# A convolution-attention and Mamba stack on one core: the last depthwise part and the last norms in turn, and the second scan step's input read from SBUF

## The chip, the core and the metric

The kernel runs on one core of a Trainium2 chip: TensorE (PE in the profile, with its weight loads as PEld), VectorE (DVE), ScalarE (ACT), GpSimd (POOL) and SyncE (SP), which share an on-chip memory (SBUF), with PSUM for the results of matmuls and HBM as main memory. Each engine runs its own instructions in order. An instruction that needs another engine's result waits on a semaphore, and everything behind it on its engine waits with it. The metric is the time of one execution in microseconds, taken on the device; less is better.

## The reference

The input is an image of 64 x 64 points with 256 channels. Layer 0 is a convolution-attention block, layer 1 a bidirectional Mamba block with an expert layer behind it:

```python
x = x + conv_attention(group_norm(x))
t = tokens(x)
t = t + mamba_both_ways(layer_norm(t))
t = t + experts(layer_norm(t))
```

For the convolutions and the attention:

```python
qkv = concat(conv1x1(x), conv3x3(x), conv5x5(x))      # q, k, v: 256 channels each
qkv = depthwise3x3(qkv)
q, k = l2norm(q), l2norm(k)                           # over the 32 channels of a head
o = softmax(q @ k.T * temperature) @ v                # 8 heads, 4096 points
```

For the Mamba block, once forward and once over the reversed tokens (u is the normalised input, 512 inner channels, 16 states each):

```python
xc, z = split(u @ in_proj.T)
xc = silu(causal_conv4(xc) + conv_b)
dt, B, C = split(xc @ x_proj.T)
dt = softplus(dt @ dt_proj.T + dt_b)
h = exp(dt * A) * h + dt * B * xc                     # step by step along the tokens
y = (h * C).sum(states) + xc * D
out = (y * silu(z)) @ out_proj.T
```

## The kernel before

All arithmetic is in float32. The kernel works on chunks of 512 points (N), and there are 8 of them (NCH). Channels lie on the 128 partitions, 256 channels as two tiles (CT). Phases follow one another; each has its own pools of SBUF and PSUM, and a pool of the next phase takes over the memory of the last one, so that its first writer waits for that memory's last readers and writers. Inside the phases the order of the instructions is written out by hand (`tc.manual_schedule`).

**The convolutions' end.** `conv_phase` (from about 80 us to 650 us) goes through twelve units (`units`): a kind (k, q or v), a half of the image and a tile of channels. For each one, PE makes the convolution and its result goes to a padded tile (`pad0` and `pad1` in turn). While unit n is convolved, the generator `depthwise` of unit n - 1 is stepped: one step is one multiply-add of DVE (L551), which adds one of nine taps to `acc`; the first tap is made by ACT (L544). The last unit is the v of the lower half, second tile. Of its rows, PE makes 16 (`shared`) by nine diagonal matmuls for each of two pieces (`products`, L520); these stand ahead of the first L551 in the generator. DVE makes the rest in two halves of eight steps. After each half `turn` transposes the result on PE (L618), ACT copies it (L620) and POOL stores it (L621).

The depthwise results of q and k are normalised in groups of up to three chunks, by a chain of callbacks that `later` puts into `events` and `tick` calls, one link a tick:

- `norm_sums`: squares on ACT (L581), sums over the heads on PE (L582)
- `norm_inverse`: maximum on DVE (L589), root on ACT (L590), reciprocal on DVE (L591), and a matmul that brings the result back to all partitions (L596)
- `norm_apply`: a product on DVE (L277) for each chunk, a reordering copy on ACT (L605) and a store by POOL (L609); it then calls `norm_sums` for the next group

When the loop over the units ends, the depthwise part of the last unit (16 steps) is still to be done, and so are two groups of q (three chunks and two), of which the sums of the first stand. The kernel before finishes the first and then the others:

```python
            drain(before)
            while events:
                tick()
```

**Attention.** `attention_phase` begins with loads by SP: the first chunk of q (L901), then k and v in eighths, tile by tile (L892, L893). A first score matmul (L1006) needs the first q and the first eighth of k. The scores and the weighting by them then keep PE busy to about 1930 us. The phase's end makes x1, the residual of layer 0, in chunks.

**The scans.** `mamba_phase` goes through 16 pairs i of a chunk c and a direction d: i = 2c + d. The backward direction (d = 1) takes the chunks from the end, so i = 1 works on chunk 7. Each i has 32 slots, one for each tile of channels, group of states and pair of rows (e, k, j). A slot is one scan on DVE over 1024 elements (L1742) and one product with C (L1747); five slots in 32, the set `POOLED`, have POOL make that product (L1752). Ahead of it, ACT makes exp(dt A) (`decay`, L1719, called da below) and POOL makes dt B xc (`inflow`, L1729, called dbx). ACT also keeps the state (L1773), and PE sums over the states (L1782). After the eight slots of one e, DVE multiplies the sum with z (`close`, L1790).

While the slots of i run, the generator `prepare(i + 1)` makes the inputs of the next one, so many steps in each slot. Its steps, in order: two projections of u into xp (L1303; PE, then copies by ACT, L1331), two more (L1336), four convolutions along the tokens (PE L1349, ACT L1345), Silu (L1353), the projection to dt, B and C (PE L1358, ACT L1361), four projections to dt (PE L1378, ACT L1374 and L1375), an exponential (L1381), a rational step (L1387 to L1394), a logarithm, and pieces of dt that are stored and read again. The projections share two PSUM tiles (`mm`), so the third has to wait for the copy of the first.

How many steps each slot gives is one, except in i = 0, where `LATE` holds them back:

```python
        LATE = {0: 0, 1: 0, 2: 0, 3: 0, 4: 0, 6: 2, 7: 6, 13: 2, 14: 2, 15: 2, 16: 2}
```

For i = 0, u was loaded at the end of attention. The input of i = 1 is the norm of chunk 7, made at the scans' own start by `start()`: the tile `un`, whose last product POOL makes (L138). SP stores it to `ud` (L1634), where i = 14 reads it again, and in the fifth slot `load_u(1)` reads it back from there into the tile `u` (L1312) for `prepare(1)`:

```python
            dt_piece(0, 0, 3, ex)
            load_u(1)
            yield
```

`start()` is itself stepped, once in each of the first slots. In its fifth slot ACT also makes Silu of z (L1642).

**The experts.** `expert_phase` follows from about 3833 us to the end.

Of the kernel before, what the change touches and what calls it, by code (L numbers as in the profile page):

```python
# [61 lines left out]
def step(gen, n=1):  # L62

    for _ in range(n):
        if gen is None or next(gen, StopIteration) is StopIteration:
            return False
    return True


def drain(gen):  # L70
    while step(gen):
        pass
# [28 lines left out]
def layer_norm(cx, pool, new_psum, src, dst, mul=None, rest=0, centred=False):  # L101

    nc = cx.nc
    xc = src
    if not centred:  # L110
        ps = new_psum()
        for t in range(CT):
            nc.tensor.matmul(ps, cx.mean_mat, src[:, t, :], start=t == 0, stop=t == CT - 1)
        yield "DVE"
        xc = pool.tile([P, CT, N], FP, name="ln_xc", tag="ln_xc", bufs=1)
        nc.vector.tensor_tensor(xc, src, ps[:, None, :].to_broadcast([P, CT, N]), ALU.subtract)
    yield "ACT"
    nc.scalar.activation(dst, xc, AF.Square)
    yield "PE"
    ps = new_psum()  # L120
    for t in range(CT):
        nc.tensor.matmul(ps, cx.mean_mat, dst[:, t, :], start=t == 0, stop=t == CT - 1)
    yield "ACT"
    rstd = pool.tile([P, N], FP, name="ln_rstd", tag="ln_rstd", bufs=1)
    nc.scalar.activation(rstd[0:1, :], ps[0:1, :], AF.Identity, bias=cx.eps[0:1, :])
    row = cx.rows.tile([1, N], FP, name="ln_row", tag="ln_row", bufs=2)
    nc.sync.dma_start(out=row, in_=rstd[0:1, :])
    few = pool.tile([P, N // P], FP, name="ln_few", tag="ln_few", bufs=1)
    nc.sync.dma_start(out=few, in_=row.rearrange("o (p j) -> (o p) j", p=P))
    for at in range(1 + rest):  # L130
        yield "POOL" if at == rest else "DMA"
    nc.gpsimd.tensor_tensor(few, few, cx.minus_half, ALU.pow)  # L132
    inv = cx.rows.tile([1, N], FP, name="ln_inv", tag="ln_inv", bufs=2)
    nc.sync.dma_start(out=inv.rearrange("o (p j) -> (o p) j", p=P), in_=few)
    nc.sync.dma_start(out=rstd, in_=inv.to_broadcast([P, N]))
    for at in range(1 + rest):
        yield "POOL" if at == rest else "DMA"
    (mul or nc.vector).tensor_tensor(dst, xc, rstd[:, None, :].to_broadcast([P, CT, N]), ALU.mult)  # L138
    yield "ACT"
# [34 lines left out]
def conv_phase(cx, xT, w1, w3, w5, temp, qd, kd, vd, uk, uv):  # L174
# [17 lines left out]
    with ExitStack() as ctx:  # L192
# [318 lines left out]
        def diagonal(ch):  # L511
            for tap in range(9):
                w_ap = wdw[:, 9 * ch + tap : 9 * ch + tap + 1]
                nc.scalar.activation(diag[:, tap, :], cx.ident, AF.Copy, scale=w_ap)
# [108 lines left out]
        rows_left, busy, events, clock = [], [], [], [0]  # L623
# [4 lines left out]
        def tick():  # L628

            clock[0] += 1  # L630
            due = [f for n, f in events if n <= clock[0]]
            events[:] = [(n, f) for n, f in events if n > clock[0]]
            for f in due:
                f()

        with tc.manual_schedule(engines=ORDERED):
# [95 lines left out]
            before = None  # L732
            for n, (kind, half, t) in enumerate(units):
# [42 lines left out]
                before = depthwise(kind, half, t, pad)  # L776
                if n == len(units) - 2:
                    diagonal(2 * CT + units[-1][2])
            drain(before)
            while events:  # L780
                tick()

# [435 lines left out]
def mamba_phase(cx, early, w_in, w_x, w_out, w1, w2, x1d, ud, bcd, dtd, x2d, u2d, usum):  # L1220
# [12 lines left out]
    with ExitStack() as ctx:  # L1233
# [60 lines left out]
        def mm_psum():  # L1294
            return pmm.tile([P, N], FP, name="mm", tag="mm")
# [13 lines left out]
        def load_u(i):  # L1309
            c, d = divmod(i, 2)  # L1310
            u = early.new_u()
            nc.sync.dma_start(out=u, in_=ud[NCH - 1 - c if d else c])  # L1312
            gots[i] = {"u": u}

        def in_pair(q, e):
            return [in_proj(q % 2, gots[q]["u"], e), in_proj(q % 2, gots[q]["u"], e + 1)]

        def few():
            return sp.tile([P, N], FP, name="few", tag="few", bufs=3)
# [228 lines left out]
        def start():  # L1548


            got, xp = gots[0], early.xp
            x1 = tl.tile([P, CT, N], FP, name="x1", tag="a1b")
            nc.gpsimd.dma_start(out=x1, in_=x1d[NCH - 1])
            un = tl.tile([P, CT, N], FP, name="un", tag="hn")
            norm = layer_norm(cx, tl, tl_psum, x1, un, nc.gpsimd)
            nc.scalar.copy(halo[0], xp[:, :, N : N + 3])
            xc = got["xc"] = pr.tile([P, ET, N], FP, name="xc", tag="xc")
            nc.scalar.activation(xc, xp[:, :, 0:N], AF.Silu)
            for d in range(2):
                nc.scalar.activation(aneg[d], cx.col(f"alog{d}", 0, ET * DS), AF.Exp)  # L1560

                nc.vector.tensor_scalar(aneg[d], aneg[d], -1.0, -1e-30, ALU.mult, ALU.min)
            nx = DR + 2 * DS
            pd = mm_psum()
            for e in range(ET):
                nc.tensor.matmul(pd[0:nx, :], wx[0][:, e, :], xc[:, e, :], start=e == 0, stop=e == ET - 1)
            xd = few()[0:nx, :]
            nc.scalar.copy(xd, pd[0:nx, :])
            nc.sync.dma_start(out=bcd[0], in_=xd[DR:nx, :])
            load_bc(0, 0)  # L1570
            ex = early.wide("ex")[:, :, 0:N]
            dt = got["dt"] = sp.tile([P, ET, N], FP, name="dt", tag="dt")

            def soft(e):
                ps = mm_psum()
                nc.tensor.matmul(ps, wdt[0:DR, P * e : P * e + P], xd[0:DR, :], start=True, stop=True)
                nc.scalar.activation(ex[:, e, :], ps, AF.Abs, bias=cx.col("dtb0", e))
                nc.vector.tensor_scalar(dt[:, e, :], ps, cx.col("dtb0", e), 0.0, ALU.add, ALU.max)
                nc.scalar.activation(ex[:, e, :], ex[:, e, :], AF.Exp, scale=-1.0)

            def rest(e):

                rd = few()
                nc.vector.tensor_scalar(rd, ex[:, e, :], -1.0, -1.0, ALU.mult, ALU.add)
                nc.vector.scalar_tensor_tensor(rd, rd, 1.0, ex[:, e, :], ALU.add, ALU.add)
                nc.vector.tensor_tensor(dt[:, e, :], dt[:, e, :], rd, ALU.add)

            def log(e):
                nc.scalar.activation(ex[:, e, :], ex[:, e, :], AF.Ln, bias=1.0)

            soft(0)
            rest(0)
            log(0)
            for v in range(2):
                dt_piece(0, v, 0, ex, nc.vector)
            load_dt(0, 0, 0)
            load_dt(0, 0, 2)
            load_bc(0, 1)

            step(norm)  # L1600
            step(norm)
            soft(1)
            step(norm)
            soft(2)
            rest(1)
            soft(3)
            step(norm)
            inflow(0)
            decay(0)
            decay(1)  # L1610
            rest(2)
            rest(3)
            step(norm)
            load_bc(0, 2)
            zs = in_pair(0, ET)
            for e in range(1, ET):
                log(e)
            inflow(1)
            step(norm)
            load_bc(0, 3)  # L1620
            yield

            for h in range(2):
                z = sp.tile([P, 2, N], FP, name="z", tag="z", bufs=3)
                got.setdefault("z", []).append(z)
                for f in range(2):
                    nc.scalar.copy(z[:, f, :], zs[f])
                if h == 0:
                    zs = in_pair(0, ET + 2)
                    for v in range(2):  # L1630
                        dt_piece(0, v, 1, ex)
                    yield
            step(norm)
            nc.sync.dma_start(out=ud[NCH - 1], in_=un)  # L1634
            drain(norm)
            yield
            dt_piece(0, 0, 2, ex)
            yield
            dt_piece(0, 1, 2)
            yield  # L1640
            for z in got["z"]:
                nc.scalar.activation(z, z, AF.Silu)  # L1642
            dt_piece(0, 0, 3, ex)
            load_u(1)
            yield
            dt_piece(0, 1, 3)
            yield
# [61 lines left out]
        gots, bcs, dts, m_of, das, us, ys, hs = {}, {}, {}, {}, {}, {}, {}, {}  # L1709
# [87 lines left out]

        AHEAD = 5

        LATE = {0: 0, 1: 0, 2: 0, 3: 0, 4: 0, 6: 2, 7: 6, 13: 2, 14: 2, 15: 2, 16: 2}  # L1800
        LONG = {1, 9, 17, 24}

        FULL = {
# [7 lines left out]
        with tc.manual_schedule(engines=ORDERED):  # L1811
# [5 lines left out]
            for n, (i, e, k, j) in enumerate(slots):  # L1817
# [40 lines left out]
                if i == 0:  # L1858
                    step(begin)
                step(prep, LATE.get(at, 1) if i == 0 else 1)  # L1860
                if at >= SPS - AHEAD and i + 2 < 2 * NCH:
# [347 lines left out]
```

## Time and profile before

| | |
|---|---|
| three runs | 4153.34, 4162.94 and 4164.72 us; median 4162.94 |
| the profiled execution's own time | 4161.68 us |
| its span, first instruction to last | 4159.7 us |
| PE busy | 3626.1 us (87%) |
| DVE busy | 3493.0 us (84%) |
| ACT busy | 2662.3 us (64%) |
| POOL busy | 1748.0 us (42%) |

All times below are microseconds from the start of the span. A line of a timeline gives the start, the time taken, the engine, the line of the kernel, the operation, the result and its inputs with their shapes, and how many instructions are merged in it. In square brackets is the time that the engine was idle before it, and what ended that wait. A float32 matmul of 512 columns stands as two records. A line of SP (SPq) is the issue of a DMA, not the transfer. Where a wait has several causes, the bracket names the one that came last.

### The profile page before, as it was taken

Reading aid. Unit: us, or ns where it says so; the run is one execution under the profiler, and the core shown is the slowest. Engines: PE = TensorE matmul, PEld = TensorE weight load, DVE = VectorE, ACT = ScalarE, POOL = GpSimd, SP = SyncE. Lnnn points to the kernel's source line nnn. Section 1 sums busy time; section 2 is a strip of 40 time slices with the busy share of each in tenths; the row PEclk is TensorE's granted clock in tenths of the full one; section 3 lists DMA queues with packets and bytes.
Section 4 is the critical chain, followed back from the end, with each engine's and each line's share of the span. In section 5 each row is a group of like instructions: output and inputs, shape, how many; then the busy total and the mean of one; then the engine's idle time right before and its main releaser. Section 6 shows DMA issues by size and latency. Waiting matters only on the chain. (4 is left out here: it accounts for less than half of the span.)

```text
span 4159.7 us, 43569 instructions
## 1 busy us (share of the span) xinstructions
PE 3626.1 (87%) x15116; PEld 1187.8 (29%) x15116; DVE 3493.0 (84%) x2898; ACT 2662.3 (64%) x4131; POOL 1748.0 (42%) x1188
## 2 busy tenths in 40 slices
PE   6769997999999999998788888888888888876798
PEld 2223332222222222222222222222222222221343
DVE  8998786889879879778899999999999999998211
ACT  1111226878878878776777778778787877774122
POOL 3020000000000000001888889888888989886000
PEclk9889998999999999999888888998989899987899
DMA  6232214000000000002334344343434334341121
GB/s 207 91 110 94 68 57 136 9 29 19 17 24 19 17 24 19 11 22 86 112 115 127 120 125 130 117 133 112 133 109 123 120 122 142 107 136 65 66 67 39
DMA packets 150533, 351.20 MB, mean 84 GB/s; under 512 B 35493, under 2 KB 44453, under 8 KB 150046
## 3 DMA queue, kind: packets, MB, share of 16 engines
q1 hardware_dynamic: 139214, 313.17, 24.5%
q0 software_dynamic: 11088, 35.14, 2.5%
q8 instruction: 121, 1.98, 0.2%
q14 instruction: 110, 0.90, 0.1%
HBM read 268.69 MB, written 79.56 MB: 84 GB/s over the span
## 5 line engine op out<-in xcount | busy, mean ns | idle before, releaser
L1729 POOL TENSOR_TENSOR dbx<-dtxr,b 128x1024 f32<-128x1024 f32 x512 | 1202.4, 2358 | 197.0 <-DMA dtxr<-dtd 97.0
L1013 ACT ACTIVATE e<-sc 128x1024 f32<-128x1024 f32 x1024 | 992.6, 1023 | 200.6 <-PE sc L1006 161.9
L1742 DVE TENSOR_TENSOR_SCAN da<-da,state,dbx 128x1024 f32<-128x1024 f32 x432 | 1014.3, 2348 | 18.2 <-ACT da L1719 7.2
L932 DVE TENSOR_TENSOR s<-s,e 128x1024 f32<-128x1024 f32 x768 | 880.8, 1221 | 43.3 <-ACT e L1013 42.8
L1719 ACT ACTIVATE da<-dtr,aneg 128x512 f32<-128x512 f32 x1024 | 708.1, 692 | 33.2 <-DMA dtr<-dtd 3.6
L1006 PE MATMUL sc<-q,kS 32*128 32x512 f32 x4096 | 652.8, 643 | 15.3 <-DMA kS<-kd 8.3
L132 POOL TENSOR_TENSOR ln_few<-ln_few,minus_half 128x4 f32<-128x4 f32 x29 | 29.4, 1014 | 1410.0 <-DMA ln_few<-ln_row 1410.0
L1747 DVE TENSOR_TENSOR h<-da,c 128x1024 f32<-128x1024 f32 x432 | 529.2, 1225 | 33.9 <-DVE da L1742 1.4
L939 PE MATMUL av<-e,vT 128*32 128x512 f32 x4096 | 548.4, 606 | 3.7 <-ACT o L945 3.7
L1782 PE MATMUL y<-h,sel 128*32 128x512 f32 x2048 | 377.1, 661 | 95.7 <-DVE h L1747 69.8
L453 PE MATMUL cv<-v,u 128*128 128x512 f32 x928 | 412.9, 605 | 28.4 <-DVE pad L274 14.0
L1303 PE MATMUL mm<-u,win 128*128 128x512 f32 x496 | 272.5, 701 | 85.4 <-ACT state L1773 29.1
L1006 PEld LDWEIGHTS sc<-q,kS 32*128 32x128 f32 x4096 | 211.5, 183 | 460.7 <-issue 235.8
L551 DVE SCALAR_TENSOR_TENSOR acc<-pad,wdw_s,acc 128x768 f32<-128x768 f32 (+1 forms) x192 | 236.2, 1235 | 24.0 <-ACT acc L544 18.3
L453 PEld LDWEIGHTS cv<-v,u 128*128 128x128 f32 x928 | 178.9, 194 | 260.0 <-issue 227.1
L1773 ACT COPY state<-da 128x2 f32<-128x2 f32 x431 | 67.9, 158 | 260.1 <-DVE h L1747 258.9
L1349 PE MATMUL mm<-xp,taps 128*128 128x512 f32 x480 | 213.3, 596 | 0.2 <-DVE m L1498 0.2
L932 DVE TENSOR_TENSOR s<-e 128x1024 f32<-128x1024 f32 x128 | 151.1, 1222 | 66.5 <-ACT e L1013 66.4
L1742 DVE TENSOR_TENSOR_SCAN h<-da,state,dbx 128x1024 f32<-128x1024 f32 x80 | 187.5, 2344 | 9.5 <-ACT state L1773 9.0
L939 PEld LDWEIGHTS av<-e,vT 128*32 128x32 f32 x4096 | 81.2, 108 | 395.5 <-issue 377.1
L1752 POOL TENSOR_TENSOR h<-h,c 128x1024 f32<-128x1024 f32 x80 | 188.3, 2354 | 2.1 <-ACT state L1773 2.1
L1303 PEld LDWEIGHTS mm<-u,win 128*128 128x128 f32 x496 | 106.5, 224 | 252.2 <-issue 109.9
(352 smaller groups left out, 3845.3 us busy)
## 6 DMA issues: line engine op xcount, KB each, us to landing
dtr<-dtd SPq DMA_DIRECT2D x128, 512.0 KB
dtxr<-dtd SPq DMA_DIRECT2D x128, 512.0 KB
b<-bcd SPq DMA_DIRECT2D x64, 256.0 KB
c<-bcd SPq DMA_DIRECT2D x64, 256.0 KB
dtd<-dt SPq DMA_DIRECT2D x64, 256.0 KB
dtd<-few SPq DMA_DIRECT2D x64, 256.0 KB
u<-uv SPq DMA_DIRECT2D x24, 640.0 KB
u<-ud SPq DMA_DIRECT2D x16, 512.0 KB
```

The lines of the kernel that those rows point to most:

```text
L453: nc.tensor.matmul(rows4(ps), u[:, dy, P * ci : P * ci + P], v[:, dy : dy + HR, ci, :], start=dy + ci == 0, stop=dy == k - 1 and ci == CT - 1,
L551: nc.vector.scalar_tensor_tensor(o, src, w_ap, o, ALU.mult, ALU.add)
L932: nc.vector.tensor_tensor(z, x, y, ALU.add)
L939: nc.tensor.matmul(g.av[32 * h : 32 * h + 32, :], vT[:, kb, P * t + 32 * h : P * t + 32 * h + 32], es[h // 2][:, h % 2, :], start=kb == 0, ...
L1006: nc.tensor.matmul(ps[h // 2][:, h % 2, :], kS[r, t, P * kb : P * kb + P], q_t[r, t, :], start=True, stop=True,)
L1013: nc.scalar.activation(e, ps[i], AF.Exp)
L1303: nc.tensor.matmul(ps, win[d][:, t, P * e : P * e + P], u[:, t, ::-1] if d else u[:, t, :], start=t == 0, stop=t == CT - 1,)
L1719: nc.scalar.activation(da[:, v, :], dts[i, e, j][0][:, v, :], AF.Exp, scale=aneg[i % 2][:, a : a + 1])
L1729: nc.gpsimd.tensor_tensor(u, dts[i, e, j][1], bcs[i, k][0][:, None, :].to_broadcast([P, 2, N]), ALU.mult)
L1742: nc.vector.tensor_tensor_scan(das[n].rearrange("p v n -> p (v n)"), da.rearrange("p v n -> p (v n)"), u.rearrange("p v n -> p (v n)"), st ...
L1747: nc.vector.tensor_tensor(h, da, bcs[i, k][1][:, None, :].to_broadcast([P, 2, N]), ALU.mult)
L1782: nc.tensor.matmul(ys[i, e][32 * j : 32 * j + 32, :], cx.sel, hs[n + j // 2][:, j % 2, :], start=False, stop=k == SQ - 1,)
```

## The change

The change makes three edits.

1. In `conv_phase`, the last unit's depthwise part and the remaining links of the norms are given out in turn: one tick, then four steps of `depthwise`, until both are done.
2. In `start()`, `un` is given to `prepare(1)` as its u as soon as the tile exists, and `load_u(1)` is left out. The store to `ud` remains.
3. `LATE` is changed to match. The first step of `prepare(1)` comes in slot 4, not 5; the next two in slot 5, not 6. By slot 7 ten steps are done, not nine, Silu of xc comes in slot 11, not 12, and from slot 17 on the count is the same as before.

```diff
@@ conv_phase
-            drain(before)
-            while events:
+
+            left = True
+            while left or events:
                 tick()
+                for _ in range(4):
+                    left = left and step(before)
@@ mamba_phase, start
             norm = layer_norm(cx, tl, tl_psum, x1, un, nc.gpsimd)
+            gots[1] = {"u": un}
             nc.scalar.copy(halo[0], xp[:, :, N : N + 3])
...
             dt_piece(0, 0, 3, ex)
-            load_u(1)
             yield
@@ mamba_phase
-        LATE = {0: 0, 1: 0, 2: 0, 3: 0, 4: 0, 6: 2, 7: 6, 13: 2, 14: 2, 15: 2, 16: 2}
+        LATE = {0: 0, 1: 0, 2: 0, 3: 0, 5: 2, 6: 2, 7: 5, 15: 2, 16: 2, 17: 2}
```

In the built program this moves instructions as follows. On DVE the order at the convolutions' end becomes L589, L591, four L551, three L277, four L551, L589, L591, four L551, two L277, four L551. On PE the three L596 of the first group come ahead of the 36 records of L520; the sums (L582) and L596 of the second group come after them, and the transposes (L618) last. On ACT the root (L590) of the first group comes ahead of the two L544. In the scans' first step POOL's order is the same as before; on ACT and PE the projections, convolutions and Silu of `prepare(1)` stand one slot earlier among the da and the sums, and SP has one DMA less.

## The prediction

> **What bounds the kernel now.** I read the page first. Its chain of waits breaks off 11 us before the end, so it can't say what the middle of the kernel hangs on. I took the stretches by time instead, then the engines' timelines at the two places that the change touches. Columns of the stretches: PE, PEld, DVE, ACT and POOL busy (instructions), granted PE clock, DMA share, GB/s.
>
> ```profile
> 622.00:651.00 29.00, 11.23 (x36) 3.95 (x34) 10.91 (x9) 9.07 (x15) 4.86 (x9) 0.59 0.19 72
> 651.00:659.00 8.00, 0.23 (x4) 0.26 (x8) 4.01 (x20) 2.01 (x2) 1.08 (x2) 0.50 0.83 259
> ...
> 1993.00:2042.00 49.00, 43.41 (x114) 13.90 (x114) 36.90 (x22) 30.48 (x54) 37.57 (x18) 0.81 0.30 98
> ...
> 2300.00:2600.00 300.00, 253.65 (x729) 83.13 (x729) 290.17 (x176) 235.66 (x462) 266.18 (x168) 0.90 0.43 126
> ```
>
> The scans (1970 to 3833 us) are DVE's: 290 of 300 us busy once they run. Two stretches are nobody's. From 622 to 651 no engine is busy for 40%: a chain hands work round. In the first scan step (1993 to 2042) DVE is busy for 36.9 of 49 us. The change works on both. First the convolutions' end, on DVE, PE and SP:
>
> ```profile
> 605.86 16.71 DVE L551 SCALAR_TENSOR_TENSOR acc<-pad,wdw_s,acc 128x768 f32<-128x768 f32 x16 [4.04 <-ACT acc L544]
> 622.48 0.68 DVE L589 TENSOR_SCALAR rn<-ps 96x512 f32<-96x512 f32 x1
> 631.43 3.35 DVE L591 RECIPROCAL rn<-rn 96x512 f32<-96x512 f32 x1 [8.26 <-ACT rn L590]
> 636.94 1.88 DVE L277 TENSOR_TENSOR acc<-acc,ps 128x512 f32<-128x512 f32 x3 [2.16 <-PE ps L596]
> ```
>
> ```profile
> 606.90 15.76 PE L520 MATMUL cv<-pad,diag 128*128 128x512 f32 x36
> ...
> 634.83 2.09 PE L596 MATMUL ps<-rn,pick_q 32*128 32x512 f32 x6 [4.37 <-DVE rn L591]
> ...
> 648.43 2.07 PE L596 MATMUL ps<-rn,pick_q 32*128 32x512 f32 x4 [4.91 <-DVE rn L591]
> 658.77 3.78 PE L1006 MATMUL sc<-q,kS 32*128 32x512 f32 x12 [8.27 <-DMA kS<-kd]
> ```
>
> ```profile
> 650.66 0.80 SPq L901 DMA_DIRECT2D q<-qd  x2
> ```
>
> The reader is to see that all 16 multiply-adds run first, and only then the two norms, one step at a time. Attention's first load goes out at 650.66, as the last broadcast of the norms (L596) ends at 650.50; its first score starts 8.1 us after that. Then the first scan step on DVE:
>
> ```profile
> 1992.77 2.36 DVE L1742 TENSOR_TENSOR_SCAN da<-da,state,dbx 128x1024 f32<-128x1024 f32 x1 [1.87 <-ACT state L1773]
> ...
> 2000.71 2.36 DVE L1742 TENSOR_TENSOR_SCAN da<-da,state,dbx 128x1024 f32<-128x1024 f32 x1 [0.68 <-ACT da L1719]
> ...
> 2007.62 0.69 DVE L1790 TENSOR_TENSOR xc<-y,z 128x512 f32<-128x512 f32 x1 [3.23 <-PE y L1782]
> ...
> 2022.26 2.36 DVE L1742 TENSOR_TENSOR_SCAN da<-da,state,dbx 128x1024 f32<-128x1024 f32 x1 [2.40 <-ACT da L1719]
> ...
> 2028.31 2.36 DVE L1742 TENSOR_TENSOR_SCAN da<-da,state,dbx 128x1024 f32<-128x1024 f32 x1 [2.36 <-ACT da L1719]
> ...
> 2033.73 2.36 DVE L1742 TENSOR_TENSOR_SCAN da<-da,state,dbx 128x1024 f32<-128x1024 f32 x1 [1.73 <-ACT da L1719]
> ...
> 2041.93 0.69 DVE L1790 TENSOR_TENSOR xc<-y,z 128x512 f32<-128x512 f32 x1 [0.92 <-PE y L1782]
> ```
>
> ```profile
> 1993.39 8.51 PE L1303 MATMUL mm<-u,win 128*128 128x512 f32 x16 [6.52 <-DMA u<-ud]
> ```
>
> These are slots 6, 8, 9, 13, 14, 15 and 17 of the first 32; the waits add up to 13.2 us. Only this PE line waits for the load that is removed.
>
> **What the Trainium skill says.** "TensorE: Matmul & The Clock Gate", What's actually happening: after an idle window of about 3.4 us PE's clock is halved, until it has been busy as long. The trace agrees: the same eight records take 5.40 us after 3.5 us of idle (at 1971.39) and 3.67 after 1.75 (at 2079.97). "ScalarE: Activation LUTs", What ACT_TABLE_LOAD costs: 1283 ns a load, plus a drain. The trace shows 1.28 and no drain beside it. "DMA: Bandwidth & Descriptors", Issuing engines are not separate DMA queues: transfers of SP and POOL share the same 16 engines. The trace has those at 0.83 busy while attention's first loads run, with POOL's last stores among them.
>
> **Part 1, the convolutions' end.** Nothing is added or removed but the order: one tick of the norms, then four multiply-adds. I follow it from 606.97, when the three sums of squares (L582) end in both kernels.
> - max 0.68, root 0.63, reciprocal 3.35 and three hand-offs: 611.8. ACT's first products (L544) now stand behind the root, and DVE's multiply-adds behind the reciprocal.
> - PE: three broadcasts 2.09, then the 36 records of the diagonal products 15.76; half a microsecond for a cold start: 630.2. The two sums of squares of the next norm now stand behind these: 631.3.
> - DVE meanwhile: four multiply-adds (16.71 / 16 = 1.04 each, 4.2), three products 1.88, four more 4.2: 622.0. Then it waits for PE until 631.3. This 9 us is the new wait; eight multiply-adds are queued behind it.
> - max, root, reciprocal 4.7: 636.0; four multiply-adds 640.1; two products 1.28 (their broadcasts ran on PE beside): 641.4; four multiply-adds: 645.5.
>
> In the built program the first load waits for the last multiply-add (it frees pad) and the last broadcast, so it goes at 645.6, not 650.66: 5.1 us less. Transposes and their copies follow until 648 and hide under the load (the first score waits for them, but at 653). POOL's last stores move into the load's first microseconds: two of qo (512 KB) before, and now 384 KB of vs as well. At the 259 GB/s of that stretch this is 1.5 us if kS waits for all of it, nothing if it is spread; I take 0.5. Stores of vd and the late taps come 15 us ahead of their readers: nothing. Part 1: 4.6 us less, between 3 and 6. Attention runs on PE without a break, so the lead stays.
>
> **Part 2, the scans' input.** SP loses one DMA (0.39 us, with 3 us to the next), which hides nothing: the next load, dtr at 1992.69, waits for ACT. POOL's order is unchanged. PE's first eight records need un alone (POOL wrote it at 1981.5) and run at 1986.9, after the sums of y, cold: 5 us. The steps of the preparation move one slot up. What that does to each wait:
> - Slot 6 (1.87): ACT ran Silu with two table loads from 1986.55 to 1991.23. Not touched: stays.
> - The two copies of xp now come before da of slot 7: 1995.6, needed at 1996.4. Free.
> - Slot 8 (0.68): POOL's dbx, one unbroken row since 1981, ends at 2000.45: 0.5 stays.
> - Slot 9 (3.23): PE starts the third projection when a copy frees its PSUM (1993.5), two projections 3.5, sums 1.06: 1998.05. But now both first convolutions (3.65 each) stand ahead of the sums that DVE waits for: 2006.4 instead of 2007.5. 2.3 stays.
> - Slot 13 (2.40): the last convolution ends at 2013.5, not 2020.1. Silu with its two loads (4.7) therefore comes ahead of da 13, which ends at 2022.0. The wait becomes 3.3: ACT again.
> - Slots 14, 15, 17 (2.36, 1.73, 0.92): Silu and the cold wx matmuls (6.06) are over at 2025.2, da 15 at 2027.5 for a scan at 2029.2. All go, 5.0.
> - Slot 19: Exp (1.91) now stands ahead of da 19: 0.3 is new.
>
> Waits left: 1.9 + 0.5 + 2.3 + 3.3 + 0.3 = 8.3 of 13.2. Part 2: 4.9 us less, between 3 and 7. Behind it DVE has next to no wait (2300 to 2600), so this lead stays too.
>
> **Sum.** 4161.68 (the profiled execution's own time, span 4159.7) - 4.6 - 4.9 = 4152.2. That execution is 1.3 us under the median of the three shown, 4162.94. I forecast 4152.
>
> **Rivals.**
> 1. Half of it: the stores delay kS by the full 1.5 and the first scan step gains only at slots 14 to 17, minus 2 for a longer Silu wait: 3.6 + 3 = 6.6 or less, 4156 to 4161. For it: four of the seven waits have another releaser than the load. Against: the count above.
> 2. More: all waits after slot 6 go (13.2 - 1.9 = 11.3) and the loads go at 644 with no delay (6.5): 4144. It needs the sums of y ahead of the convolutions, which the order of PE's instructions speaks against.
> 3. Slower. The diagonal products now follow a 5 us idle on PE. Were all 36 records at half clock (31.5 us for 15.76), the sums come at 647, the last multiply-add at 661.3, the load 10.7 later than before; less 4.9, the kernel is 5.8 slower: 4167.5. The point is 5 + 4.9 = 9.9 us lost at this place. Against: an unbroken row of 15 us warms within its first quarter. With a loss in the scans as well it could pass 12.5.
> 4. The change does nothing measurable because a later wait takes the lead back. Against: no fixed time lies behind; every load is issued from the same order.
>
> **Numbers.** About 0.3% (12.5 us) is what a measurement of this kernel can tell from none; the three runs span 11 us. Forecast (4148 to 4156) 0.55; rival 1 0.22; rival 2 0.13; rivals 3 and 4 0.10. My gain is under the bound, so most of it counts as no change; faster by over 0.3% (under 4150.5) has rival 2 and, with the runs' spread, a quarter of the forecast: 0.28. Slower by over 0.3%: 0.06. Range: gains of 11.5 and 3, and the runs' spread, about 7 and 3: 4143 to 4161.
>
> **What would show it.** First load about 645.6 and first score about 654; DVE idle some 9 us before the second max of rn; in the scans 2 us left before the first product with z, 3 before slot 13, next to none at 14 to 17. Wrong if the first score starts after 657 or slot 20 runs less than 3 us early against slot 0.

## The result, and the profile after

The kernel after takes 4154.15 us, the median of 20 runs (4148.2 to 4161.31); the kernel before, beside it, 4163.32 (20 runs, 4151.93 to 4165.9). The ratio is 0.9982, with a 95% interval of 0.9975 to 0.9988: by this ratio 7.5 us less, between 5.0 and 10.4. (The two medians lie 9.2 apart, the two means 7.2; the runs of before are spread wider.) The prediction had 9.5 less. The profiled execution has a span of 4151.9 us, where that of before had 4159.7.

The same stretches as before, in the kernel after; columns are PE, PEld, DVE, ACT and POOL busy (instructions), granted PE clock, DMA share, GB/s:

```profile
622.00:651.00 29.00, 19.65 (x54) 8.68 (x53) 17.03 (x23) 7.08 (x13) 3.83 (x8) 0.79 0.16 54
651.00:659.00 8.00, 3.82 (x14) 1.28 (x12) 1.68 (x10) 1.68 (x3) 1.07 (x2) 0.50 1.04 362
1993.00:2042.00 49.00, 40.16 (x114) 11.88 (x113) 39.91 (x24) 33.65 (x58) 39.44 (x19) 0.82 0.25 78
2300.00:2600.00 300.00, 257.48 (x728) 83.40 (x728) 292.23 (x177) 237.03 (x463) 268.11 (x167) 0.89 0.42 130
```

The chain between 622 and 651 is denser, since part of the diagonal products and multiply-adds now falls into it: PE 19.65 us busy instead of 11.23, DVE 17.03 instead of 10.91. Between 1993 and 2042 DVE does 39.91 instead of 36.9; the scans begin 4.7 us earlier here, so these are not quite the same slots. The long stretch behind it is as full as before. In the timelines, first the convolutions' end on DVE:

```profile
609.62 0.69 DVE L589 TENSOR_SCALAR rn<-ps 96x512 f32<-96x512 f32 x1 [5.28 <-PE ps L582]
...
620.06 4.17 DVE L551 SCALAR_TENSOR_TENSOR acc<-pad,wdw_s,acc 128x768 f32<-128x768 f32 x4
634.19 0.68 DVE L589 TENSOR_SCALAR rn<-ps 64x512 f32<-64x512 f32 x1 [9.96 <-PE ps L582]
...
644.02 4.17 DVE L551 SCALAR_TENSOR_TENSOR acc<-pad,wdw_s,acc 128x768 f32<-128x768 f32 x4
```

then on PE and SP:

```profile
616.51 16.63 PE L520 MATMUL cv<-pad,diag 128*128 128x512 f32 x36
633.07 1.05 PE L582 MATMUL ps<-sq,heads 128*32 128x512 f32 x4
...
655.46 3.78 PE L1009 MATMUL sc<-q,kS 32*128 32x512 f32 x12 [4.18 <-DMA kS<-kd]
```

```profile
648.36 0.80 SPq L904 DMA_DIRECT2D q<-qd  x2
```

The order is that of the plan. DVE waits 9.96 us for sums of squares that stand behind 36 diagonal products. In this execution the convolutions were 2.6 us later already ahead of the changed place (the first group's sums end at 609.59, at 606.97 in before), so distances from there are compared: the first load comes 38.8 us after these sums (43.7 before), the first score 45.9 (51.8 before).

The first scan step on DVE:

```profile
1982.24 2.35 DVE L1745 TENSOR_TENSOR_SCAN h<-da,state,dbx 128x1024 f32<-128x1024 f32 x1 [1.24 <-POOL dbx L1732]
...
1998.90 2.36 DVE L1745 TENSOR_TENSOR_SCAN da<-da,state,dbx 128x1024 f32<-128x1024 f32 x1 [1.97 <-POOL dbx L1732]
...
2004.33 0.69 DVE L1793 TENSOR_TENSOR xc<-y,z 128x512 f32<-128x512 f32 x1 [1.74 <-PE y L1785]
...
2019.52 2.36 DVE L1745 TENSOR_TENSOR_SCAN da<-da,state,dbx 128x1024 f32<-128x1024 f32 x1 [2.95 <-ACT da L1722]
...
2043.03 2.36 DVE L1745 TENSOR_TENSOR_SCAN da<-da,state,dbx 128x1024 f32<-128x1024 f32 x1 [2.16 <-ACT da L1722]
```

These are slots 4, 8, the product with z ahead of 9, 13 and 19. Slots 14 to 17 have no wait any more, and PE no longer waits for a load:

```profile
1982.90 5.78 PE L1306 MATMUL mm<-un,win 128*128 128x512 f32 x8
1991.20 3.70 PE L1306 MATMUL mm<-un,win 128*128 128x512 f32 x8 [2.52 <-ACT xp L1334]
```

Slot 19 is new and larger than foreseen. Why, ACT shows:

```profile
2035.65 0.69 ACT L1377 ACTIVATE ex<-mm,small 128x512 f32<-128x512 f32 x1 [2.18 <-PE mm L1381]
...
2038.35 1.90 ACT L1384 ACTIVATE ex<-ex 128x2048 f32<-128x2048 f32 x1
2040.28 0.63 ACT L1390 ACTIVATE few<-ex 128x512 f32<-128x512 f32 x1
2040.94 0.63 ACT L1391 ACTIVATE few<-few 128x512 f32<-128x512 f32 x1
...
2041.52 1.42 ACT L1722 ACTIVATE da<-dtr,aneg 128x512 f32<-128x512 f32 x2
```

ACT waits 2.18 us for the last projection to dt (L1381), which stands behind sums of y on PE; then da 18, Exp and two small operations come ahead of da 19 (the last line). And PE is slow there:

```profile
2022.96 1.12 PE L1381 MATMUL mm<-few,wdt 16*128 16x512 f32 x2
...
2029.68 2.07 PE L1381 MATMUL mm<-few,wdt 16*128 16x512 f32 x2 [3.55 <-ACT dt L1378]
2031.67 1.94 PE L1785 MATMUL y<-h,sel 128*32 128x512 f32 x8
2033.54 2.07 PE L1381 MATMUL mm<-few,wdt 16*128 16x512 f32 x2
```

From 2029.68 to 2035.54, behind 3.55 us of idle time, the granted clock is 0.50; at 2022.96, where the same product takes 1.12, it is 1.00.

How far the first scan step has come is read best from the start of x, the last sum of attention's x1 (L918 before, L921 after), to the scan of slot 20: 109.81 us before, 106.98 after, 2.8 less.

### The profile page after: what moved, and what is told of

The parts are those of the page before. It is cut to its first block, busy times and chain, and to the rows that moved or that the text cites. A ratio compares the mean times of both kernels' runs of the same rounds, so it can differ in the third digit from the quotient of the medians.

```text
span 4151.9 us, 43571 instructions
## 1 busy us (share of the span) xinstructions
PE 3628.4 (87%) x15116; PEld 1187.3 (29%) x15116; DVE 3490.2 (84%) x2898; ACT 2663.5 (64%) x4131; POOL 1749.4 (42%) x1188
## 5 line engine op out<-in xcount | busy, mean ns | idle before, releaser
L1306 PE MATMUL mm<-u,win 128*128 128x512 f32 x464 | 251.4, 692 | 79.6 <-ACT z L1413 29.6
L551 DVE SCALAR_TENSOR_TENSOR acc<-pad,wdw_s,acc 128x768 f32<-128x768 f32 (+1 forms) x192 | 236.0, 1234 | 19.9 <-ACT acc L544 14.2
L942 PEld LDWEIGHTS av<-e,vT 128*32 128x32 f32 x4096 | 81.2, 108 | 396.0 <-issue 378.4
L1785 PEld LDWEIGHTS y<-h,sel 128*32 128x32 f32 x2048 | 57.2, 113 | 379.4 <-DVE h L1750 161.5
```

The source lines that it names most:

```text
L551: nc.vector.scalar_tensor_tensor(o, src, w_ap, o, ALU.mult, ALU.add)
L942: nc.tensor.matmul(g.av[32 * h : 32 * h + 32, :], vT[:, kb, P * t + 32 * h : P * t + 32 * h + 32], es[h // 2][:, h % 2, :], start=kb == 0, ...
L1306: nc.tensor.matmul(ps, win[d][:, t, P * e : P * e + P], u[:, t, ::-1] if d else u[:, t, :], start=t == 0, stop=t == CT - 1,)
L1785: nc.tensor.matmul(ys[i, e][32 * j : 32 * j + 32, :], cx.sel, hs[n + j // 2][:, j % 2, :], start=False, stop=k == SQ - 1,)
```

## The experiments

Theory after the result: part 1 brings what the prediction says, part 2 less, since slot 19 takes half of its gain back. Rivals: all the gain comes from one place; or the table of steps alone, or the load alone, makes part 2. All eleven kernels were timed beside the kernel before. "Load" and "score" are the first load of q and the first score, from the end of the first group's sums of squares; "x to 20" and "8 to 20" are distances to the scan of slot 20. All of these come from one profiled execution each, and that need not be a typical one: e8's took 4145.38 us, 8 under its median.

| run | median us (before beside it) | ratio, 95% interval | load | score | x to 20 | 8 to 20 |
|---|---|---|---|---|---|---|
| before | | | 43.7 | 51.8 | 109.8 | 51.2 |
| after | 4154.15 (4163.32) | 0.9982, 0.9975 to 0.9988 | 38.8 | 45.9 | 107.0 | 47.7 |
| e1_conv_only | 4156.65 (4162.48) | 0.9985, 0.9979 to 0.9992 | 39.4 | 48.1 | 111.1 | 51.3 |
| e2_scan_only | 4159.6 (4162.48) | 0.9994, 0.9987 to 1.0 | 44.2 | 51.7 | 109.1 | 48.9 |
| e3_un_old_late | 4161.19 (4162.48) | 0.9999, 0.9991 to 1.0007 | 43.8 | 52.4 | 108.0 | 49.0 |
| e4_late_with_load | 4162.83 (4162.48) | 1.0001, 0.9992 to 1.001 | 44.2 | 52.8 | 112.7 | 48.9 |
| e5_conv_front | 4150.47 (4161.61) | 0.9972, 0.9963 to 0.9982 | 36.7 | 45.3 | 106.2 | 47.9 |
| e6_sums_first | 4152.56 (4161.61) | 0.9981, 0.9973 to 0.9989 | 39.6 | 47.9 | 108.2 | 49.9 |
| e7_dt_early | 4149.9 (4161.61) | 0.997, 0.9961 to 0.998 | 39.3 | 48.2 | 106.1 | 47.3 |
| e8_all | 4153.35 (4161.61) | 0.998, 0.9973 to 0.9986 | 36.3 | 44.7 | 108.3 | 49.3 |
| e9_front_squares | 4146.41 (4161.25) | 0.9966, 0.9952 to 0.998 | 35.2 | 43.9 | 106.0 | 47.7 |
| e10_front_squares_dt | 4144.9 (4161.25) | 0.9958, 0.9945 to 0.9972 | 33.6 | 39.7 | 105.9 | 47.8 |
| e11_front_seven | 4152.07 (4161.25) | 0.9976, 0.9969 to 0.9983 | 37.6 | 43.8 | 106.9 | 48.9 |

### The two parts alone

e1_conv_only is the kernel before with edit 1; e2_scan_only the kernel before with edits 2 and 3.

> Only the convolutions' end is in turn; the scans are those of the kernel before. Theory: the two parts of the change do not meet, so this kernel gains part 1 alone: 4.6 us by the prediction, up to 5.9 by the trace of the kernel after (first score 45.9 us after the sums of squares, 51.8 before); slot 0 to slot 20 of the scans as long as before. Rival: the first score is early, but attention or the norm behind it takes the lead back: less than 2 us. Second rival: the whole 9 us of the kernel after comes from here: 8 us or more.

> Only the scans' second input and their table are changed; the convolutions end as before. Theory: the lead at slot 20 against the scans' start, 2.8 us in the trace of the kernel after, is what reaches the end: 2 to 4 us. The prediction had 4.9 (3 to 7). Rival: the 1.9 to 2.2 us by which the scans started earlier in the kernel after belong to this part: then 5 us or more, with the distance from x to scan 0 at 26.5 us again and not 28.6.

e1 takes 6.2 us less (3.3 to 8.7) by its ratio, e2 2.5 less (0 to 5.4). Together that is 8.7, beside 7.5 for the whole change: within the intervals the parts add up. The first is the larger by its middle value; the intervals overlap, and that of e2 reaches down to nothing. In e1 the long wait and the load stand as in the kernel after:

```profile
631.43 0.68 DVE L589 TENSOR_SCALAR rn<-ps 64x512 f32<-64x512 f32 x1 [10.60 <-PE ps L582]
```

```profile
645.60 0.80 SPq L903 DMA_DIRECT2D q<-qd  x2
```

The expectation that e1's scans take as long as before held from slot 8 on (51.3 us, 51.2 before), and not from slot 0 (84.8, 81.2 before). In e1, e2 and the kernel after, slot 0 comes 26.3 to 26.5 us after x, in before and e3 28.4 to 28.6. Since e1 has the scans of before, this belongs to no part of the change. It brings nothing either: slot 8 comes 58.6 us after x in before, 59.9 in e1, 60.2 in e2, 59.3 after. (Over all thirteen traces slot 0 comes 24.9 to 29.8 us after x, and slot 8 still 58.0 to 60.2, but for e4 with 63.8.) What starts earlier waits in slots 3 to 8 for POOL's dbx and ACT. The rival of e2 falls with that.

### The load or the table?

Both have edit 1 undone. e3_un_old_late has edit 2 with the old `LATE`:

```diff
-        LATE = {0: 0, 1: 0, 2: 0, 3: 0, 5: 2, 6: 2, 7: 5, 15: 2, 16: 2, 17: 2}
+        LATE = {0: 0, 1: 0, 2: 0, 3: 0, 4: 0, 6: 2, 7: 6, 13: 2, 14: 2, 15: 2, 16: 2}
```

e4_late_with_load has the new `LATE`, with `load_u(1)` left in place and `un` not handed over.

> The second scan takes its input from SBUF, but the preparation keeps the old table of steps. Theory: most waits of the first scan step hung on the late load, so this alone gains about 3 us (1.5 to 4.5): the waits ahead of slots 9, 13, 15 shrink, and Silu with its two table loads stands ahead of the scan of slot 14 with a wait of about 3 us. Rival: the new table makes the gain and the load is hidden: 0 to 1 us.

> The new table of steps, but the input is still stored and loaded again. Theory: the projections wait for the load until about 1993 us of the profile as before, now with two convolutions of 3.65 us ahead of the sums that DVE waits for instead of one: the wait ahead of the first product with z grows from 3.2 to 5 us or more, slots 14 to 17 lose their waits: no change, between 2 us faster and 3 us slower. Rival: the table makes the gain and the load is hidden: 3 us or more faster.

Neither can be told from the kernel before by its time. Their intervals overlap that of e2 too, so what follows is read from the traces. e3 on DVE, at the product with z, and slots 13 and 14:

```profile
2006.88 0.69 DVE L1791 TENSOR_TENSOR xc<-y,z 128x512 f32<-128x512 f32 x1 [0.99 <-PE y L1783]
...
2021.52 2.36 DVE L1743 TENSOR_TENSOR_SCAN da<-da,state,dbx 128x1024 f32<-128x1024 f32 x1 [2.40 <-ACT da L1720]
...
2027.57 2.36 DVE L1743 TENSOR_TENSOR_SCAN da<-da,state,dbx 128x1024 f32<-128x1024 f32 x1 [2.36 <-ACT da L1720]
```

and on ACT, ahead of da 13:

```profile
2019.37 0.69 ACT L1346 ACTIVATE xc<-mm,small 128x512 f32<-128x512 f32 x1 [3.40 <-PE mm L1350]
```

Without the load the first product with z waits 0.99 us instead of 3.23. But the wait at slot 13 is 2.40, as in before: ACT takes the last convolution's result in slot 11's step, ahead of da 13, and PE has that convolution behind sums of y, until 2019.3. The waits of slots 14 and 15 stay too (2.36 and 2.00). My expectation that these shrink was wrong: they hang on the table, not on the load. e4, on DVE, PE and ACT:

```profile
2003.74 2.36 DVE L1742 TENSOR_TENSOR_SCAN da<-da,state,dbx 128x1024 f32<-128x1024 f32 x1 [5.75 <-ACT da L1719]
```

```profile
1995.22 9.72 PE L1303 MATMUL mm<-u,win 128*128 128x512 f32 x16 [6.80 <-DMA u<-ud]
```

```profile
1999.01 0.59 ACT L1331 COPY xp<-mm 128x512 f32<-128x512 f32 x1 [4.67 <-PE mm L1303]
```

The table takes the waits of slots 14 to 17 away (8 to 20: 48.9), but its copies of xp now stand ahead of da 7 on ACT and wait for the load with PE: 5.75 us at slot 7. I had expected that at the product with z, which waits 3.00, as in e2. Each edit alone brings 2 us behind slot 8; the table pays for its share with a wait at slot 7 unless the load is gone. What the table adds once the load is gone is not shown: e3, without it, has 49.0 from slot 8 and 108.0 from x, and the five traces with both edits have 47.7 to 48.9 and 106.0 to 109.1.

### The wait behind the diagonal products

e5_conv_front is the kernel after with the products first:

```diff
-            left = True
+            left, turns = step(before), [8]
             while left or events:
                 tick()
-                for _ in range(4):
+                for _ in range(turns.pop() if turns else 4):
```

> The kernel after, but one multiply-add step (and so the 36 diagonal products) is put ahead of the first turn of the norms, and eight stand behind the first turn. Theory: DVE's 9.96 us wait is made by the order on PE alone, the 36 products of 16.6 us standing ahead of the sums of squares. Put first they start as the sums end, at 15.8 us on a warm PE, and DVE does its multiply-adds beside them: the first load goes 32 us after the end of the sums of squares of the first norm (38.8 and 39.4 in the two traces with the turns), the first score 39 after: about 6.5 us faster than the kernel after, 12 to 15 us (0.3%) faster than before. Rival: the wait is the norms' own chain of root, reciprocal and broadcast, or ACT's queue: the load stays within 2 us of 39 and the gain is that of the turns alone, 5 to 6 us on the convolutions' side.

The load comes 36.7 us after the sums, 2 to 3 us earlier than with the turns, not 7: the theory was right on where the 9.96 us came from, and wrong that they would be free. DVE, and ACT ahead of the second group's sums:

```profile
624.07 1.88 DVE L277 TENSOR_TENSOR acc<-acc,ps 128x512 f32<-128x512 f32 x3 [4.92 <-PE ps L596]
...
635.22 0.68 DVE L589 TENSOR_SCALAR rn<-ps 64x512 f32<-64x512 f32 x1 [5.17 <-PE ps L582]
```

```profile
629.37 2.92 ACT L605 COPY qo<-acc 128x512 f32<-128x512 f32 x3
632.07 1.14 ACT L581 ACTIVATE sq<-acc 128x512 f32<-128x512 f32 x2
```

The wait has split: 4.92 us for the broadcasts, now behind the products on PE, and 5.17 us for the sums, whose squares stand behind ACT's copies. The next runs take the second half apart. e11_front_seven gives seven steps behind the first tick, so that the transposes and evacuations come behind the norms' products; e9_front_squares also issues the squares ahead of the three copies, for every group of the norms:

```diff
             for (a, kind, t, c), ps in zip(chunks, back):
                 plus(a, a, ps, ALU.mult)
+            norm_sums()
+            for (a, kind, t, c), ps in zip(chunks, back):
                 if kind == "q":
...
-            norm_sums()
```

> As the run with the products first, but seven multiply-adds behind the first turn, not eight (the transposes then stand behind the norms' products), and the squares of the next norm are issued ahead of the three copies of the norm before. In that run 9.96 us of one wait had come back as 4.92 (broadcasts behind the diagonal products) and 5.17 (squares behind ACT's copies). Theory: the second is ACT's queue, 2.9 us of copies and some 3 us of evacuations ahead of the squares: with these behind, DVE's second wait falls under 1.5 us, the first load goes 32 to 34 us after the end of the sums of squares (36.7 there, 39.3 with the turns), the first score 41 to 42 after (45.3 there). Rival: the squares wait for the products with the broadcasts, whatever ACT does: the load stays at 36 or more.

> The run with the products first, seven multiply-adds instead of eight behind the first turn, the squares still behind the copies. Theory: only the evacuations go behind the squares, the 2.9 us of copies stay ahead: the load 34 to 35.5 us after the end of the sums of squares, between the two others. Rival: the copies are what counts, or the evacuations alone: as one of the two others within 0.7 us.

e9, the same two waits and the one behind them:

```profile
621.60 1.88 DVE L277 TENSOR_TENSOR acc<-acc,ps 128x512 f32<-128x512 f32 x3 [4.31 <-PE ps L596]
...
627.49 0.68 DVE L589 TENSOR_SCALAR rn<-ps 64x512 f32<-64x512 f32 x1
631.45 3.34 DVE L591 RECIPROCAL rn<-rn 64x512 f32<-64x512 f32 x1 [3.29 <-ACT rn L590]
```

The wait for the sums is gone, as expected. In its place the reciprocal waits 3.29 us for the root, which now stands behind ACT's evacuations. So it was ACT's queue, but the wait moved within it: the load comes at 35.2 in e9, neither at the 32 to 34 that I expected nor at the rival's 36, and the score at 43.9 instead of 41 to 42. In e10, which has the same convolutions, the load comes at 33.6; one microsecond of that is PE's clock, since the diagonal products take 16.82 us in e9 and 15.82 in e10 (see part 1 below). In e11 the same wait is larger, and the load, at 37.6, later than in e5 and than the 34 to 35.5 that I had put:

```profile
636.00 3.35 DVE L591 RECIPROCAL rn<-rn 64x512 f32<-64x512 f32 x1 [6.01 <-ACT rn L590]
```

### The waits left in the scans

e6_sums_first and e7_dt_early change the kernel after by one entry or two of the table:

```diff
-        LATE = {0: 0, 1: 0, 2: 0, 3: 0, 5: 2, 6: 2, 7: 5, 15: 2, 16: 2, 17: 2}
+        LATE = {0: 0, 1: 0, 2: 0, 3: 0, 5: 2, 6: 2, 7: 3, 8: 3, 15: 2, 16: 2, 17: 2}   # e6
+        LATE = {0: 0, 1: 0, 2: 0, 3: 0, 5: 2, 6: 2, 7: 5, 14: 2, 15: 2, 17: 2}         # e7
```

> The kernel after with three steps of the preparation moved from slot 7 to slot 8, so that both first convolutions stand behind the sums of y that DVE's first product with z waits for. Theory: that wait (1.74 and 3.00 us in the two traces with the new table, 0.99 with one convolution ahead) falls under 0.8, slot 20 comes 1 to 2 us earlier against the start of the stage, the time 1 to 2 us under the kernel after. Rival: the convolutions are then late by as much and slot 13 waits for ACT longer by as much: slot 20 the same within 0.7 us.

> The kernel after with one step of the preparation moved from slot 16 to slot 14, so that the last product with wdt stands ahead of the second sums of y on PE. Theory: slot 19's 2.16 us come from ACT's wait of 2.18 us for that product, with Exp and two more operations behind it: the wait goes under 0.6 us and slot 20 comes 1.5 us or more earlier. Rival: ACT is short of time by itself there, and the wait moves to slots 15 to 18: slot 20 the same within 0.7 us.

e6 on DVE and PE:

```profile
2010.59 2.35 DVE L1745 TENSOR_TENSOR_SCAN h<-da,state,dbx 128x1024 f32<-128x1024 f32 x1 [2.26 <-ACT da L1722]
2014.48 2.36 DVE L1745 TENSOR_TENSOR_SCAN da<-da,state,dbx 128x1024 f32<-128x1024 f32 x1 [1.54 <-ACT da L1722]
```

```profile
2001.13 14.01 PE L1352 MATMUL mm<-xp,taps 128*128 128x512 f32 x32
```

The product with z waits no more, but all four convolutions now run in one row of 14 us, ACT takes each result ahead of a da, and slots 10 and 11 wait 3.8 us: 8 to 20 is 49.9 us, 1.7 more than in the mean of the five traces with the change's own table. In the trace the gain I expected is a loss; by its time e6 (0.9981) can't be told from the kernel after (0.9982). The rival was right that the wait returns, and had the wrong slot. e7 has no wait at slot 18 and 1.54 at 19 (2.57 together after), with another cause on ACT:

```profile
2040.01 1.42 ACT L1722 ACTIVATE da<-dtr,aneg 128x512 f32<-128x512 f32 x2 [1.56 <-DVE h L1745]
```

da 19 now waits for PSUM that the scan of slot 18 frees; 8 to 20 is 47.3, against 47.7 to 48.9 in the five traces that have the change's own table. ACT's wait of 2.18 us is gone, so the cause was named rightly; but the wait came back in part, and its worth was one microsecond, not the 1.5 expected. By its time e7 is 12.5 us faster than before (8.3 to 16.2), more than slot 20 shows: its profiled execution is another 5.3 us shorter behind slot 20 than that of after (2100.0 us from there to the end, 2105.3). That stays open. From the third on, the scan steps of all these traces take 113.0 to 120.3 us each, whatever the edit, so I put none of it down to this one.

### Together

e8_all is e5 with both moves of the table, e10_front_squares_dt is e9 with that of e7 alone.

> The order of the convolutions' end of the run with the products first, and both moved steps of the preparation. Theory: the three gains add up: 6.5 + 1.5 + 1.5 us under the kernel after, 15 to 19 us (0.4%) faster than before. Rival: only the convolutions' part shows: 11 to 14 us faster than before.

> The run before with the one step of the preparation moved from slot 16 to slot 14 as well. Theory: the two add up, with slot 20 one us earlier against the start of the stage than in the run before, and the time 13 to 17 us (0.3 to 0.4%) under the kernel before: the fastest of all. Rival: no more than the run before, within 1 us.

e8 brings 8.3 us (5.8 to 11.2), less than both stories. By the traces the move of e6 costs about 2 us (108.3 from x to 20, 106.2 in e5), and the products first bring 2 to 3 at the load, not 6.5. e10 is the fastest of all: 17.5 us less than before (11.7 to 22.9), 0.42%. Its first load and first score:

```profile
637.59 0.80 SPq L905 DMA_DIRECT2D q<-qd  x2
```

```profile
643.70 2.09 PE L1010 MATMUL sc<-q,kS 32*128 32x512 f32 x8 [2.40 <-DMA kS<-kd]
```

The score comes 7.8 us earlier than in the mean of the four runs with the turns of the change (47.5), which with the change's own 7.5 makes 15.3. Some of this may be chance: the load is 5.7 earlier, and the other 2.1 are a shorter way from load to score (6.1 us here and in e11, 8.7 in e9), for which no cause is shown. The further microsecond at slot 20 isn't there (105.9 from x, 106.0 in e9). Between e9 and e10 the intervals overlap.

## Why the prediction was right, and where it was off

**Part 1, 4.6 us: right.** Two sets of traces can be put side by side: before, e2, e3 and e4 with the old order, after, e1, e6 and e7 with the turns. The load comes 43.99 us after the sums in the first (mean), 39.28 in the second: 4.7 us earlier, where the prediction had 5.1. The first score goes from 52.18 to 47.50: 4.7 earlier. The steps:
- The wait of 9 us for PE behind the diagonal products: 9.96 and 10.60.
- 15.76 us and half a microsecond for the diagonal products after an idle PE: 16.63, 17.27, 17.49 and 17.14 in the four, 16.20 in the mean of the nine others, so 0.93 more, not 0.5. "TensorE: Matmul & The Clock Gate", What's actually happening, has a window of about 3.4 us until the clock is full again; counted from the broadcasts (2.08) just ahead, that would leave 1.3 us at half speed, an estimate of 0.7 lost. But the same section calls the window free-running, so it need not start with the broadcasts, and the granted clock (third column from the right) shows that it didn't. In after:

```profile
616.51:618.37 1.86, 1.86 (x5) 0.83 (x3) 1.82 (x3) 0.00 (x0) 0.00 (x0) 0.50 0.00 0
618.38:633.14 14.76, 14.76 (x37) 6.35 (x37) 5.75 (x7) 3.98 (x5) 1.62 (x3) 1.00 0.14 53
```

The row is at half clock for its first 1.86 us here, 3.17 in e1, 3.61 in e6, 2.90 in e7, and 0.1 to 2.3 in the nine others. In each of the thirteen traces it takes 15.7 us and half of that time. Rival 3, with all 36 records at half clock, fell: even in e6 13.9 of 17.49 us are at the full one.
- The 0.5 us for POOL's stores beside the load of kS: not seen. From load to score it is 8.19 us in the mean of the first four and 8.22 in that of the second; single traces have 7.1 to 8.9, so half a microsecond could hide there.

The time agrees: 6.2 us for e1, with 4.6 inside its interval.

**Part 2, 4.9 us: the direction right, the size too large by the traces.** By e2's time it is 2.5 us (0 to 5.4), an interval that holds 4.9 as well. From x to slot 20 it is 3.4 us: 110.5 in the mean of before and e1, 107.0 in that of after, e2, e5, e9 and e11, which have exactly this table, each with its own scatter (106.0 to 109.1 in the five). The prediction's table of waits, term by term; e5 stands beside the kernel after because its slot 0 comes as long after x as in before (28.6 us both), which the prediction took for granted:

| wait, us | before | predicted | after | e5 |
|---|---|---|---|---|
| slots 3 to 5 | none | none | 2.93 | none |
| slot 6 | 1.87 | 1.9 | 0.1 | 1.86 |
| slot 8 (7 and 8) | 0.68 | 0.5 | 2.14 | 0.50 |
| product with z | 3.23 | 2.3 | 1.74 | 1.96 |
| slot 13 | 2.40 | 3.3 | 2.95 | 2.95 |
| slots 14, 15 and second product | 5.01 | 0 | 0 | 0 |
| slots 18 and 19 | none | 0.3 | 2.57 | 2.57 |
| sum | 13.2 | 8.3 | 12.4 | 9.8 |

- Slots 13 to 17 came as worked out: Silu and its two table loads once, 2.95 us, and 5 us gone. In e5 slots 6 and 8 did too. The product with z waits 1.74 to 3.00 us in the five traces, 2.3 in their mean.
- The term that was mis-sized is slot 19: "Exp (1.91) now stands ahead of da 19: 0.3 is new" was 2.57 with slot 18. I counted Exp and not what stands around it: ACT's wait of 2.18 us for the last projection to dt, and the two small operations behind Exp. That is 2.3 us more than put down. PE's half clock is enough to explain ACT's wait: at the 1.12, 1.06 and 1.12 us that these records take at 2022.96 to 2026.12, the row from 2029.68 would end 2.8 us sooner, by an estimate from these lines. No run tests that apart.
- That the waits of the kernel after add up to nearly as much as before, and the stage is yet shorter, is no contradiction. In after, slot 0 started 2.2 us earlier against x, as in e1, and the waits of slots 3 to 5 give that back. The prediction took slots 0 to 7 as fixed against slot 0; slot 8 is nearer to fixed against x, and the waits ahead of it are for POOL's row of dbx and for ACT. Its own test, slot 20 against slot 0, therefore fails in after (80.5 us, 81.2 before, where it asked for 3 less), and holds in e5 and e9 (77.7 both), whose slot 0 comes 28.6 and 28.3 us after x.

**The sum.** 4.7 + 3.4 = 8.1 from the traces, 7.5 (5.0 to 10.4) by the time, 9.5 predicted. That the forecast lies within 2 us does not show its terms: slot 19 was 2.3 off, and smaller misses at slot 13 and at the product with z took back 0.7 of that (in e5). Of the rivals, the first (half of it) had part 2 near its size, 3 us, for another reason, and the time doesn't exclude its 6.6; but the delay of kS by the stores, on which it rests for part 1, is not seen. The second fell: the sums of y did not come ahead of the convolutions, and e6, which puts them there, shows no gain. The fourth fell: e1, with part 1 alone, is 3.3 to 8.7 us faster.

## What to carry to other kernels

When two chains share an in-order engine, dealing them out in turn moves the wait instead of removing it: look for the longest row on each engine (here 36 matmuls) and ask what of the other chain stands behind it, then ask it again of the next engine; here the wait went from PE's products to ACT's copies and then to ACT's evacuations, and each move freed only part of it. A step moved into an earlier slot brings along whatever its consumer on another engine waits for: Exp, charged at its own 1.9 us, came with 1.3 us of small operations behind it and a wait of 2.2 us ahead. Where a row of matmuls follows idle time, look at the granted clock over it: here the same 36 records took 15.8 to 17.5 us, by when the clock turned full. Compare executions by distances from a common event ahead of the change, and take several traces of the same order: single waits in the filling of a pipeline shift by 2 us without any edit.

## What was not expected of the hardware

The 2.2 us between slot 0 in before and in after come from two operations of DVE just ahead of it. In before, on DVE and POOL:

```profile
1964.25 0.69 DVE L1586 TENSOR_TENSOR dt<-dt,few 128x512 f32<-128x512 f32 x1
...
1965.32 2.72 DVE L1585 SCALAR_TENSOR_TENSOR few<-few,ex 128x512 f32<-128x512 f32 x1
1968.07 2.72 DVE L1586 TENSOR_TENSOR dt<-dt,few 128x512 f32<-128x512 f32 x1
```

```profile
1964.90 5.34 POOL L1729 TENSOR_TENSOR dbx<-dtxr,b 128x1024 f32<-128x1024 f32 x2 [17.54 <-DMA dtxr<-dtd]
```

The same operation takes 0.69 us alone and 2.72 beside POOL's products, each about as long as one of POOL's two (2.67). In after only one of them, at 1963.42, fell beside POOL; the other took 0.69. "SBUF — State Buffer", Who interferes with whom, says that a DVE instruction with two inputs in SBUF contends with a GpSimd instruction that reads SBUF; both do here, and the trace agrees.
